# Softmax sums of an attention layer for two units at once, in four column strips

## The chip, the cores and the metric

The kernel runs on one core of a Trainium2 chip. The core has TensorE (matmuls, PE in the profile), VectorE (DVE), ScalarE (ACT), GpSimd (POOL) and SyncE (SP), which issues the DMAs. The metric is the device time of one execution in microseconds (us); lower is better. The kernel's time is a median over several runs. The profile is of one further execution.

## The reference

Eight images of 384 channels and 32 x 32 pixels pass four layers, each of the form x = x + layer(groupnorm(x)), in float32: a convolutional attention (layer 0), a mixture of four experts (layer 1), a quantised depthwise-separable convolution (layer 2) and a deformable attention (layer 3). The change is inside layer 3's attention. With 6 heads of 64 channels, 1024 queries (the pixels) and 256 keys (sampled positions), cut to what matters:

```python
    qh = q.reshape(B, NUM_HEAD, DIM_HEAD, H * W).transpose(0, 1, 3, 2)
    ...
    attn = jax.nn.softmax(jnp.einsum('bhqd,bhkd->bhqk', qh, k) * SCALE, axis=-1)
    out = jnp.einsum('bhqk,bhkd->bhqd', attn, v)
    out = out.transpose(0, 1, 3, 2).reshape(B, DIM, H, W)
    out = jnp.einsum('bchw,oc->bohw', out, proj_w) + proj_b[None, :, None, None]
```

So each query needs the sum of 256 exponentials, and the 64 outputs of its head are divided by that sum.

## The kernel before

The whole program is one launch. Layer 0 runs first, layer 1 of the images follows, and the last stage, in which the change lies, is a loop over the images b = 0 to 6: layers 2 and 3 of image b, written as a generator, are interleaved with layer 1 of image b + 1, which is cut into small units of TensorE work (groups of the ph matmuls, L1481, and of the y matmuls, L1502). Each `yield` of the generator adds its number to a budget, and for every 2.6 (`UNIT`) in it one unit of layer 1 is issued. The order in which instructions are issued is therefore the order on each engine. Image 6 runs beside image 7's layers 2 and 3, and image 7 (`last`) ends alone.

Layer 3's attention of an image is cut into six units: three head pairs `pr` times two halves `h` of 512 queries. One unit is made of these steps:

- `scores` (L1800): four matmuls, keys on the partitions and two heads side by side, into two large PSUM tiles.
- `exps` (L1817): two ScalarE exponentials of 128 x 1024, tiles p.
- p01 (L1862): GpSimd adds the two tiles, so that only 128 rows are left to be summed.
- `weigh` (L1826): four matmuls, p times v, into one PSUM bank pav; the two heads take 64 rows each. There is one such bank (`vbank`).
- tu (L1874): VectorE transposes pav in 32 x 32 blocks into an SBUF tile, which frees the bank.
- `sums` (L1839): two matmuls with a 128 x 64 block of ones, one for each head, write the sums into a bank pss (from `fbank`, three banks); each sum stands in 64 equal rows.
- `divide`: VectorE transposes pss (ts, L1847), takes the reciprocal of one column in each block (L1849, 128 x 16, kept in rec3), multiplies tu by it (L1850) and transposes the product into att (L1853).

The sums and the division of a unit are issued one unit late (`due3`): behind the next unit's weigh and, on VectorE, behind its tu. After the sixth unit come its own sums and division, and then the projection pf (L1929), x (L1937) and the output's DMA (L1944). Beside the tail VectorE starts the layer 1 of image b + 2: x<-o (L1427) with tiles o that a DMA loads (L1411) into buffers of the pool that also holds p and p01, and ScalarE makes h from x (L1430). Further VectorE work there is y's addition to x (L1508), its statistics (L106, L111) and x<-w0s (L1454).

rec3 keeps all reciprocals of all images; at the end of the program a check of their range reads it (outside the usual range a general version runs again).

Of the kernel before, what the change touches and what calls it, by code (L numbers as in the profile page):

```python
# [7 lines left out]
F32 = mybir.dt.float32  # L8
# [6 lines left out]
P = 128  # L15
KC = C // P
HALF = N // 2
# [38 lines left out]
def tile_kernel(ctx: ExitStack, tc: tile.TileContext, i: dict, out: bass.AP):  # L56
    nc = tc.nc
# [33 lines left out]
    ones = const.tile([P, P], F32, name="ones")  # L91
# [175 lines left out]
    with ExitStack() as pa:  # L267
# [7 lines left out]
        last = NK - 1  # L275
# [246 lines left out]
        for n, (u, kind, s) in enumerate(work):  # L522
            k, h = divmod(u, 2)
# [25 lines left out]
            else:  # L549
                two = [big(f"pk{n}_{r}") for r in range(2)]  # L550
                banks = [two[r // 2][:, r % 2 * HALF : (r % 2 + 1) * HALF] for r in range(4)]
                outs = [(t, 2 * r, 2) for r, t in enumerate(two)]
            if kind == "v":
                h, c = h + s, 0
# [5 lines left out]
            for p in passes:  # L560
                j, x = p
                c0, c1 = max(0, 1 - x), W - max(0, x - 1)
                for q in range(nq):
# [3 lines left out]
                    elif kind == "y":  # L567
                        g, j, w = s, q, slice(0, 64)
# [4 lines left out]
                    for r, rs in enumerate(quads):  # L573
                        nc.tensor.matmul(  # L574
                            banks[r][cols[q]].rearrange("p (h w) -> p h w", w=W)[:, :, c0:c1],
                            lhsT=cws[rs, c, 2 * h + g, x, w],
                            rhs=src[rs, :, c0 + x - 1 : c1 + x - 1],
                            start=(p == passes[0]), stop=(p == passes[-1]),
# [13 lines left out]
            for q in range(4):  # L592
                rows = quads[q]
                if kind == "y":
                    v, j = divmod(q, 2)
# [5 lines left out]
                else:  # L601
                    g, j = divmod(q, 2)
# [69 lines left out]
    with ExitStack() as pb:  # L672
# [192 lines left out]
        nxt = scores_of(*steps[0])  # L865
        todo.pop(0)()
        pav = None
        for n, (b, pr, h, kc) in enumerate(steps):
# [34 lines left out]
            if n + 1 < len(steps):  # L903
                nxt = scores_of(*steps[n + 1])
# [20 lines left out]
        for k in range(2):  # L925
            qs = slice(k * HALF // 2, (k + 1) * HALF // 2)
            for m in range(KC):
                for c in range(KC):
                    nc.tensor.matmul(
                        pos[m][:, qs], lhsT=wo0[:, c, m * P : (m + 1) * P],  # L930
                        rhs=atts[B - 1][:, c, HALF:][:, qs], start=(c == 0), stop=(c == KC - 1),
# [24 lines left out]
    _, sco, sho = sc_o  # L956
# [51 lines left out]
    with tc.If(redo > 0):  # L1008
        with ExitStack() as pb:
# [13 lines left out]
            with tc.For_i(0, B) as bi:  # L1023
# [11 lines left out]
                for t in range(NT8):  # L1035
                    pv = bank(f"pv_e{t}")
                    for c in range(KC):
                        nc.tensor.matmul(
                            pv[:, :C], lhsT=act[2][:, c, t * P : (t + 1) * P],
                            rhs=w_in[2][:, c, :], start=(c == 0), stop=(c == KC - 1),  # L1040
# [8 lines left out]
                for v in range(2):  # L1049
                    ts = qp.tile([P, NPAIR0, N], F32, tag=f"qk{v}", name=f"qk{v}_e")  # L1050
                    for pr in range(KC):
                        for h in range(2):
                            pq = bank(f"pq{v}_e{pr}_{h}")
                            for c in range(KC):
                                nc.tensor.matmul(
                                    pq, lhsT=w_in[v][:, c, pr * P : (pr + 1) * P],
                                    rhs=rows_of(act[v][:, c, :], h * H // 2, (h + 1) * H // 2) if v == 0
                                    else act[v][:, c, h * HALF : (h + 1) * HALF],
                                    start=(c == 0), stop=(c == KC - 1),
# [8 lines left out]
                for pr in range(NPAIR0):  # L1068
                    qt, kt = qks[0][:, pr, :], qks[1][:, pr, :]
                    for h in range(2):  # L1070
                        pav = bank(f"pav_e{pr}_{h}")
                        for j, r in enumerate(HR):
                            hd = 2 * pr + j
                            pt = qp.tile([P, NT8, HALF], F32, tag="pt", name=f"pt_e{pr}_{h}_{j}")
                            for qc in range(4):
# [3 lines left out]
                                for kh in range(2):  # L1079
# [3 lines left out]
                                        start=True, stop=True,  # L1083
# [3 lines left out]
                                p = pp.tile([P, N], F32, tag="p", name=f"p{nm}")  # L1087
# [14 lines left out]
                            for kc in range(NT8):  # L1102
# [5 lines left out]
                                    rhs=pt[:, kc, :],  # L1108
                                    start=(kc == 0),
                                    stop=(kc == NT8 - 1),  # L1110
# [49 lines left out]
    def fbank(name):  # L1160
        return ps_f.tile([P, HALF], F32, tag="f", name=name)
# [219 lines left out]
    om_dram = dram.tile([B, 3, NG * LS], F32, name="omd")  # L1381
    NU3 = 2 * NPAIR3
    rec3 = wd.tile([P, B * NU3, 16], F32, name="rec3")
    bad3 = wd.tile([P, 1], mybir.dt.int32, name="bad3")

    xs_img, started = {}, {}
# [209 lines left out]
    def layer3(pl, b, xt, put, general):  # L1596
# [196 lines left out]
        def scores(pr, h):  # L1793

            ss = []
            for kc in range(2):
                s = big(f"s3_{b}_{pr}_{h}_{kc}")
                for j in range(2):
                    r = slice(64 * j, 64 * j + 64)
                    nc.tensor.matmul(  # L1800
                        s[:, j * HALF : (j + 1) * HALF],
                        lhsT=kt[r, pr, kc * P : (kc + 1) * P],
                        rhs=q[r, pr, h * HALF : (h + 1) * HALF],
                        start=True, stop=True,
                    )
                ss.append(s)
            return ss

        def exps(u, ss):
            ps = []  # L1810
            for kc in range(2):
                nm = f"p3_{b}_{u}_{kc}"
                if last:
                    p = third(pl, 2 * (u % 2) + kc, nm).rearrange("p a n -> p (a n)")[:, :N]
                else:
                    p = pl.flat([P, N], nm)
                nc.scalar.activation(p, ss[kc], AF.Exp, scale=0.125)  # L1817
                ps.append(p)
            return ps
# [14 lines left out]
        if not general:  # L1834
            def sums(u, p01):

                pss = fbank(f"pss3_{b}_{u}")
                for j in range(2):
                    nc.tensor.matmul(  # L1839
                        pss[64 * j : 64 * j + 64, :], lhsT=ones[:, :64],  # L1840
                        rhs=p01[:, j * HALF : (j + 1) * HALF], start=True, stop=True,
                    )
                return pss

            def divide(pss, pr, h, u, tu):
                tss = pl.one([P, 16, 32], "ts", f"ts_{b}_{u}")
                nc.vector.transpose(tss.rearrange("p a b -> p (a b)"), pss)  # L1847
                rc = rec3[:, b * NU3 + u, :]
                nc.vector.reciprocal(rc, tss[:, :, 0])  # L1849
                nc.vector.tensor_tensor(  # L1850
                    tu, tu, rc.unsqueeze(2).to_broadcast([P, 16, 32]), ALU.mult
                )
                nc.vector.transpose(  # L1853
                    att[:, pr, h * HALF : (h + 1) * HALF], tu.rearrange("p a b -> p (a b)")
                )


            ps, due3 = exps(0, scores(*units[0])), None
            yield UNIT
            for u, (pr, h) in enumerate(units):  # L1860
                p01 = pl.flat([P, N], f"p01_{b}_{u}")
                nc.gpsimd.tensor_tensor(p01, ps[0], ps[1], ALU.add)  # L1862
                nxt = scores(*units[u + 1]) if u + 1 < NU3 else None
                if last and nxt:
                    nxt = exps(u + 1, nxt)
                pav = weigh(pr, h, ps)
                if due3:
                    pss = sums(due3[2], due3[4])
                if nxt:
                    ps = nxt if last else exps(u + 1, nxt)  # L1870

                tu = pl.one([P, NG * LS], f"om{u % 2}", f"tu_{b}_{u}")[:, :HALF]
                tu = tu.rearrange("p (a b) -> p a b", b=32)
                nc.vector.transpose(tu.rearrange("p a b -> p (a b)"), pav)  # L1874
                if due3:
                    divide(pss, *due3[:4])
                due3 = pr, h, u, tu, p01
                yield UNIT
                yield 0.0
            divide(sums(due3[2], due3[4]), *due3[:4])  # L1880
            yield 3.0
        else:
            for pr, h in units:
                pav = vbank(f"pav3_{b}_{pr}_{h}")
                for j in range(2):
                    r = slice(64 * j, 64 * j + 64)
                    nm = f"3_{b}_{pr}_{h}_{j}"
                    s = big(f"s{nm}").rearrange("p (a k) -> p a k", a=4)
                    for qc in range(4):
                        q0 = h * HALF + qc * P  # L1890
                        nc.tensor.matmul(
                            s[:, qc, :], lhsT=q[r, pr, q0 : q0 + P], rhs=kt[r, pr, :],
                            start=True, stop=True,
                        )
                    mx = small.tile([P, 4], F32, tag="mx4", name=f"mx{nm}")
                    nc.vector.reduce_max(mx, s, AX.X, negate=True)
                    nc.vector.tensor_scalar(mx, mx, 0.125, None, ALU.mult)
                    p = pl.flat([P, 4, LS], f"p{nm}")
                    rs = small.tile([P, 4], F32, tag="rs4", name=f"rs{nm}")
                    for qc in range(4):  # L1900
                        nc.scalar.activation(
                            p[:, qc, :], s[:, qc, :], AF.Exp, bias=mx[:, qc : qc + 1],
                            scale=0.125, accum_out=rs[:, qc : qc + 1],
                        )
                    nc.vector.reciprocal(rs, rs)
                    nc.vector.tensor_tensor(
                        p, p, rs.unsqueeze(2).to_broadcast([P, 4, LS]), ALU.mult
                    )
                    pt = pl.flat([P, 2, HALF], f"pt{nm}")
                    for kc in range(2):  # L1910
                        tp = fbank(f"tp{nm}_{kc}")
                        for qc in range(4):
                            nc.tensor.transpose(
                                tp[:, qc * P : (qc + 1) * P], p[:, qc, kc * P : (kc + 1) * P], ident
                            )
                        nc.vector.tensor_copy(pt[:, kc, :], tp)
                    hd = 2 * pr + j
                    for kc in range(2):
                        nc.tensor.matmul(
                            pav[r, :], lhsT=vt[:, kc, hd * 64 : (hd + 1) * 64], rhs=pt[:, kc, :],  # L1920
                            start=(kc == 0), stop=(kc == 1),
                        )
                nc.vector.tensor_copy(att[:, pr, h * HALF : (h + 1) * HALF], pav)
# [249 lines left out]
```

## Time and profile before

| quantity | value |
|---|---|
| median of 3 runs | 3491.53 us |
| lowest and highest run | 3490.93 and 3492.99 us |
| the profiled execution | 3494.72 us |
| its span | 3492.9 us |
| its mean granted TensorE clock | 0.987 |
| sums, L1839 | 192 records, median 592 ns |
| transpose of the sums, L1847 | 48, median 716 ns |
| reciprocal times tu, L1850 | 48, median 1300 ns, 672 to 1574 |
| addition of exponentials, L1862 | 48, mean 2355 ns |

A float32 matmul leaves two records, one for each pass; matmuls are pipelined, so that records overlap and the time of one is more than its share. In a line of the timeline the columns are the start in us from the span's start, the length of the group in us, engine, line of the kernel, operation, output and inputs, shapes, the number of records, and in brackets the idle time of the engine before it with what ended it. Times in the timeline are those of the profiled execution. A TensorE line with "128*64" has 128 rows of weights and 64 columns.

### The profile page before, as it was taken

The numbers are of one execution on the slowest core, as the hardware profiler recorded it, in microseconds if no ns is written. First come the engines' busy times: TensorE is split into PE (matmuls) and PEld (weight loads), VectorE is DVE, ScalarE is ACT, GpSimd is POOL, SyncE is SP. The second block draws the span as 40 slices with busy tenths as digits, with TensorE's granted clock in tenths as the row PEclk, the third lists the DMA queues.
The fourth block names the chain that finished last, engine by engine and source line by source line (L and its number), as shares of the span: only waits on it lengthen the run. The fifth ranks groups of instructions, "written<-read, shape, count | busy, mean of one in ns | idle before, by whom it ended". The sixth has DMA issues, their size and how long they took to land.

```text
span 3492.9 us, 44919 instructions
## 1 busy us (share of the span) xinstructions
PE 3384.1 (97%) x18599; PEld 1458.3 (42%) x18599; DVE 1696.7 (49%) x2881; ACT 1298.5 (37%) x1514; POOL 206.1 (6%) x231
## 2 busy tenths in 40 slices
PE   6999999999999999998999999999999999999888
PEld 2333434343434343443344445344453444534434
DVE  8942232323232323234366365663656637566573
ACT  5655544444444444433222323313233232232222
POOL 2100000000000000000000200102001020010112
PEclk9999999999999999999999999999999999999898
DMA  9972121212121212123500101101111011110000
GB/s 357 295 205 79 26 79 27 79 26 79 26 79 26 79 27 78 28 79 125 220 24 21 50 39 35 40 21 50 40 35 40 21 50 40 35 39 18 0 37 19
DMA packets 86259, 234.01 MB, mean 67 GB/s; under 512 B 21672, under 2 KB 21896, under 8 KB 79130
## 3 DMA queue, kind: packets, MB, share of 16 engines
q1 hardware_dynamic: 83882, 222.75, 19.9%
q10 hardware_dynamic: 1248, 4.72, 0.3%
q8 instruction: 150, 2.46, 0.3%
q0 software_dynamic: 912, 3.53, 0.3%
q14 instruction: 67, 0.55, 0.1%
HBM read 145.77 MB, written 75.59 MB: 63 GB/s over the span
## 4 chain that ended last, share of the span: by engine, by line
PE 41%; DVE 9%; DMA 1%; ACT 1%; POOL 0%; issue 0%; DVEq 0%; ACTq 0%; POOLq 0%; SPq 0%
PE y L1502 12%; PE ph L1481 10%; DVE y L1577 5%; PE pq L1622 4%; PE pw L1585 3%; PE pf L1929 3%; PE s L1800 2%; PE pav L1826 2%; DVE hd L1467 1%; DMA o<-o 1%; PE pk L1775 1%; PE pv L1784 1%; PE xsb L1761 1%; PE pss L1839 1%; PE plog L1231 1%; DVE off L1692 1%
## 5 line engine op out<-in xcount | busy, mean ns | idle before, releaser
L827 ACT ACTIVATE p<-s 128x1024 f32<-128x1024 f32 x512 | 496.3, 1021 | 365.7 <-PE s L820 365.5
L835 PE MATMUL pav<-p,vt 64*64 64x512 f32 x4096 | 494.7, 588 | 0.0
L1481 PE MATMUL ph<-h,w_sb 128*128 128x512 f32 x1104 | 486.8, 595 | 6.3 <-ACT h L1430 6.3
L1502 PE MATMUL y<-hd,w_sb 128*128 128x512 f32 x1080 | 488.7, 600 | 3.5 <-DVE hd L1467 3.5
L820 PE MATMUL s<-qk,qk 48*64 48x512 f32 x2944 | 355.1, 592 | 0.0
L1481 PEld LDWEIGHTS ph<-h,w_sb 128*128 128x128 f32 x1104 | 207.0, 190 | 267.5 <-issue 249.8
L1502 PEld LDWEIGHTS y<-hd,w_sb 128*128 128x128 f32 x1080 | 199.9, 191 | 248.2 <-issue 235.8
L835 PEld LDWEIGHTS pav<-p,vt 64*64 64x64 f32 x4096 | 168.2, 133 | 273.7 <-issue 273.4
L796 DVE COPY ta<-pav 128x512 f32<-128x512 f32 (+1 forms) x65 | 44.2, 682 | 475.5 <-PE pav L835 475.5
L1491 ACT ACTIVATE hd<-ph,b_sb 128x512 f32<-128x512 f32 x180 | 122.7, 682 | 312.7 <-PE ph L1481 312.7
L1577 DVE SCALAR_TENSOR_TENSOR y<-h,tap,y 128x961 f32<-128x961 f32 (+1 forms) x192 | 233.8, 1241 | 0.6
L574 PE MATMUL pk<-xs,cws_sb 32*32 32x496 f32 (+3 forms) x3840 | 179.4, 601 | 39.4 <-DMA xs<-in_xs_dram 24.8
L1692 DVE SCALAR_TENSOR_TENSOR off<-q,dw_sb,off 128x225 f32<-128x225 f32 (+3 forms) x432 | 211.9, 544 | 1.6
L820 PEld LDWEIGHTS s<-qk,qk 48*64 48x64 f32 x2944 | 109.1, 133 | 211.4 <-issue 190.5
L1817 ACT ACTIVATE p<-s 128x1024 f32<-128x1024 f32 x96 | 96.1, 1023 | 166.5 <-PE s L1800 141.7
L81 DVE COPY qk<-pq 128x512 f32<-128x512 f32 x46 | 31.8, 691 | 251.9 <-PE pq L258 251.9
L1467 DVE TENSOR_TENSOR hd<-hd,cb 128x512 f32<-128x512 f32 x180 | 122.3, 684 | 41.0 <-ACT hd L1491 40.8
L574 PEld LDWEIGHTS pk<-xs,cws_sb 32*32 32x32 f32 (+1 forms) x3840 | 77.7, 111 | 139.4 <-issue 54.0
L1585 PE MATMUL pw<-y,upw 128*128 128x512 f32 x288 | 129.0, 601 | 4.9 <-DVE y L1577 4.9
L1862 POOL TENSOR_TENSOR p<-p,p 128x1024 f32<-128x1024 f32 x48 | 113.0, 2355 | 349.3 <-ACT p L1817 349.3
L820 PE MATMUL s<-ql,ql 48*64 48x512 f32 x1024 | 128.3, 592 | 0.2 <-ACT p L827 0.2
L1929 PE MATMUL pf<-att,wp_sb 128*128 128x512 f32 x288 | 127.6, 598 | 0.5 <-DVE x L1937 0.5
(326 smaller groups left out, 3718.1 us busy)
## 6 DMA issues: line engine op xcount, KB each, us to landing
rqk<-y SPq DMA_DIRECT2D x96, 256.0 KB
g<-rqk SPq DMA_DIRECT2D x96, 256.0 KB
xs<-in_xs_dram SPq DMA_DIRECT2D x56, 384.0 KB
g<-rv SPq DMA_DIRECT2D x48, 256.0 KB
xh<-in_x_dram SPq DMA_DIRECT2D x48, 256.0 KB
f<-in_x_dram SPq DMA_DIRECT2D x24, 512.0 KB
f<-o SPq DMA_DIRECT2D x24, 512.0 KB
o<-ot SPq DMA_DIRECT2D x42, 256.0 KB
```

The costliest lines, as they stand in the source:

```text
L574: nc.tensor.matmul(banks[r][cols[q]].rearrange("p (h w) -> p h w", w=W)[:, :, c0:c1], lhsT=cws[rs, c, 2 * h + g, x, w], rhs=src[rs, :, c0 ...
L820: nc.tensor.matmul(s[64 * k : 64 * k + 64, j * HALF : (j + 1) * HALF], lhsT=kt[r, k0 : k0 + 64], rhs=qt[r, h * HALF : (h + 1) * HALF], sta ...
L827: nc.scalar.activation(p, s, AF.Exp, scale=scale)
L835: nc.tensor.matmul(pav[k][64 * j : 64 * j + 64, :], lhsT=vts[b % 2][r, kc, 2 * hd : 2 * hd + 2, :].rearrange("p a b -> p (a b)"), rhs=p[r, ...
L1467: nc.vector.tensor_tensor(hd, hd, state["cb"], ALU.mult)
L1481: nc.tensor.matmul(ph, lhsT=w1[:, e, c, dc * P : (dc + 1) * P], rhs=state["h1"][c], start=(c == 0), stop=(c == KC - 1),)
L1502: nc.tensor.matmul(y, lhsT=w2[:, e, dc, m * P : (m + 1) * P], rhs=state[h, k], start=(k == 0), stop=(k == NE * KC - 1),)
L1577: nc.vector.scalar_tensor_tensor(d, f, tap2[:, c, t : t + 1], d, ALU.mult, ALU.add)
L1585: nc.tensor.matmul(pw[h], lhsT=upw2[:, c, m * P : (m + 1) * P], rhs=y[c][:, hs], start=(c == 0), stop=(c == KC - 1),)
L1622: nc.tensor.matmul(pq[h], lhsT=wq3[:, c, m * P : (m + 1) * P], rhs=h3[h][:, c, :], start=(c == 0), stop=(c == KC - 1),)
L1692: nc.vector.scalar_tensor_tensor(d, f, dw3[:, t : t + 1], d, ALU.mult, ALU.add)
L1929: nc.tensor.matmul(pf[:, hs], lhsT=wp3[:, pr, m * P : (m + 1) * P], rhs=att[:, pr, hs], start=(pr == 0), stop=(pr == NPAIR3 - 1),)
```

## The change

For the images 0 to 6 the sums are made after every second unit, for two units at once. Four matmuls with a 128 x 32 block of ones write into four strips of 32 rows of one bank: two heads of two units. One transpose and one reciprocal serve both units; the reciprocal goes to a new 128 x 16 tile rc2, and eight copies of 32 x 16 bring its rows to where each unit's rows of tu need them: every strip is copied twice into rec3. Then follow multiply and transpose of each unit, as before (`turn`). The pair's sums and turns are issued after the second unit's `yield UNIT`, and so behind a unit of layer 1 if the budget holds one; the exponentials of the unit after a pair are issued behind them. Image 7 keeps the old order.

```diff
     rec3 = wd.tile([P, B * NU3, 16], F32, name="rec3")
+    rc2 = wd.tile([P, 16], F32, name="rc2")
...
+            def turn(rc, pr, h, tu):
+                nc.vector.tensor_tensor(
+                    tu, tu, rc.unsqueeze(2).to_broadcast([P, 16, 32]), ALU.mult
+                )
+                nc.vector.transpose(
+                    att[:, pr, h * HALF : (h + 1) * HALF], tu.rearrange("p a b -> p (a b)")
+                )
+
+            def divide_two(two):
+                pss = fbank(f"pss3_{b}_{two[0][2]}")
+                for k, (_, _, _, _, p01) in enumerate(two):
+                    for j in range(2):
+                        r = 64 * k + 32 * j
+                        nc.tensor.matmul(
+                            pss[r : r + 32, :], lhsT=ones[:, :32],
+                            rhs=p01[:, j * HALF : (j + 1) * HALF], start=True, stop=True,
+                        )
+                tss = pl.one([P, 16, 32], "ts", f"ts_{b}_{two[0][2]}")
+                nc.vector.transpose(tss.rearrange("p a b -> p (a b)"), pss)
+                nc.vector.reciprocal(rc2, tss[:, :, 0])
+                for k, (pr, h, u, tu, _) in enumerate(two):
+                    rc = rec3[:, b * NU3 + u, :]
+                    for j in range(2):
+                        for e in range(2):
+                            r = 64 * j + 32 * e
+                            nc.vector.tensor_copy(
+                                rc[r : r + 32], rc2[64 * k + 32 * j :][:32]
+                            )
+                    turn(rc, pr, h, tu)
+
             def divide(pss, pr, h, u, tu):
...
-                nc.vector.tensor_tensor(
-                    tu, tu, rc.unsqueeze(2).to_broadcast([P, 16, 32]), ALU.mult
-                )
-                nc.vector.transpose(
-                    att[:, pr, h * HALF : (h + 1) * HALF], tu.rearrange("p a b -> p (a b)")
-                )
-
-
-            ps, due3 = exps(0, scores(*units[0])), None
+                turn(rc, pr, h, tu)
+
+
+            ps, due3, two = exps(0, scores(*units[0])), None, []
...
-                if nxt:
+                if nxt and (last or u % 2 == 0):
                     ps = nxt if last else exps(u + 1, nxt)
...
-                due3 = pr, h, u, tu, p01
+                if last:
+                    due3 = pr, h, u, tu, p01
+                else:
+                    two.append((pr, h, u, tu, p01))
                 yield UNIT
+                if len(two) == 2:
+                    divide_two(two)
+                    two = []
+                    if nxt:
+                        ps = exps(u + 1, nxt)
                 yield 0.0
-            divide(sums(due3[2], due3[4]), *due3[:4])
+            if last:
+                divide(sums(due3[2], due3[4]), *due3[:4])
             yield 3.0
```

In the changed kernel the multiply stands in line 1847, the transpose into att in 1850, the pair's matmuls in 1859, its transpose, reciprocal and copies in 1864, 1865 and 1871, tu in 1900, and pf in 1964.

## The prediction

> **What bounds the kernel now.** I read the shares of the engines first, then the chain that ended last, then the timeline of TensorE in one attention stage, then VectorE's and GpSimd's beside it. From the page's first part and its chain:
>
> ```profile
> span 3492.9 us, 44919 instructions
> PE 3384.1 (97%) x18599; PEld 1458.3 (42%) x18599; DVE 1696.7 (49%) x2881; ACT 1298.5 (37%) x1514; POOL 206.1 (6%) x231
> PE 41%; DVE 9%; DMA 1%; ACT 1%; POOL 0%; issue 0%; DVEq 0%; ACTq 0%; POOLq 0%; SPq 0%
> ```
>
> TensorE is busy 97% of the span, so a matmul taken away shortens the run only if TensorE does not then wait. TensorE's timeline over the end of image 2's attention (start, length, engine, line, operation, count, idle before in brackets):
>
> ```profile
> 2428.12 2.84 PE L1502 MATMUL y<-hd,w_sb 128*128 128x512 f32 x6
> 2430.89 1.99 PE L1800 MATMUL s<-q,kt 64*128 64x512 f32 x8
> 2432.81 1.94 PE L1826 MATMUL pav<-p,vt 128*64 128x512 f32 x8
> 2434.57 1.03 PE L1839 MATMUL pss<-p,ones 128*64 128x512 f32 x4
> 2435.65 1.94 PE L1826 MATMUL pav<-p,vt 128*64 128x512 f32 x8
> 2437.39 1.92 PE L1839 MATMUL pss<-p,ones 128*64 128x512 f32 x8
> 2439.24 3.70 PE L1929 MATMUL pf<-att,wp_sb 128*128 128x512 f32 x8
> 2442.78 1.02 PE L1481 MATMUL ph<-h,w_sb 128*128 128x512 f32 x2
> 2444.92 1.13 PE L1481 MATMUL ph<-h,w_sb 128*128 128x512 f32 x2 [1.12 <-ACT h L1430]
> 2445.89 12.29 PE L1929 MATMUL pf<-att,wp_sb 128*128 128x512 f32 x28
> ```
>
> Groups follow without a gap except 1.12 us. One unit's sums (four records, two matmuls in two passes each) cost one slot: from one start to the next 2428.12 - 2427.16 = 0.96 us in the steady part, 1.92 for the two last units, of which 2 x 0.43 = 0.86 is streaming (592 ns of a record overlap its neighbour) and the rest is the change of shape. VectorE and GpSimd in a unit of image 1:
>
> ```profile
> 2200.84 2.35 POOL L1862 TENSOR_TENSOR p<-p,p 128x1024 f32<-128x1024 f32 x1 [5.06 <-ACT p L1817]
> ...
> 2200.54 0.72 DVE L1874 STREAM_TRANSPOSE tu<-pav 128x512 f32<-128x512 f32 x1 [3.47 <-PE pav L1826]
> 2201.40 0.72 DVE L1847 STREAM_TRANSPOSE ts<-pss 128x512 f32<-128x512 f32 x1
> 2202.15 0.25 DVE L1849 RECIPROCAL rec<-ts 128x16 f32<-128x16 f32 x1
> 2202.44 1.30 DVE L1850 TENSOR_TENSOR tu<-tu,rec 128x512 f32<-128x512 f32 x1
> 2203.77 0.71 DVE L1853 STREAM_TRANSPOSE att<-tu 128x512 f32<-128x512 f32 x1
> ```
>
> The multiply takes 1.30 us here and 0.68 after the last unit (2443.94). It ends 0.55 us after GpSimd's addition of the exponentials (2200.84 + 2.35 = 2203.19): while that addition runs, a VectorE operation with two inputs in SBUF stands still; transposes and reciprocals do not. And VectorE idles 3.47 us before a unit's turn, so in the steady part it has room.
>
> One more place shows what a long wait of TensorE costs, at the last image's attention:
>
> ```profile
> 3378.86 3.68 PE L1826 MATMUL pav<-p,vt 128*64 128x512 f32 x8 [4.23 <-DVE tu L1874]
> 3382.30 2.78 PE L1839 MATMUL pss<-p,ones 128*64 128x512 f32 x6
> ```
>
> After 4.23 us of waiting for VectorE the same eight records take 3.68 instead of 1.94 us.
>
> **What the Trainium skill says.** "TensorEngine Tiling (Array Packing)", Available Configurations and Key Properties: 128 rows by 32 columns makes four tiles that work independently, and a change of mode drains the array. The trace agrees: the gate logits (L1231), four 32-column strips, need 2.71 us for 24 records (1696.05 to the next group at 1698.76), which is 6 x 0.43 plus 0.13, and changes of shape cost 0.1 to 0.2. "VectorE: DVE Perf Modes", Two Vector instructions with no wait between them: an instruction whose input or output starts in another quadrant of 32 partitions than the last one's is held until all earlier ones have finished, and VectorE's second SBUF read interface is shared with GpSimd. The second half agrees with the multiplies above; shifted copies are not in this trace. "TensorE: Matmul & The Clock Gate", Part 1: an idle window of about 3.4 us halves the clock; the 4.23 us wait above agrees.
>
> **The change part by part**, for images 0 to 5 (one instruction order for all six), then image 6; image 7 keeps its code.
>
> 1. *Four strips.* Before, six slots per image. After: one slot for units 0 and 1, one for 2 and 3. In the third pair the first matmul of unit 4 is issued alone ahead of unit 5's pav, and the other three follow behind it: two slots again. So 6 become 4, not 3: 2 x 0.86 = 1.72 less, and all of it ahead of the point that matters (part 3). Two lone groups add a change of shape, so I take 1.6.
>
> 2. *VectorE's count.* Per pair one transpose (0.72) and one reciprocal (0.25) go; eight copies of 32 x 16 come. Nearest rows: L383's copy of 128x32, 160 ns; small steps of that kind are 0.09 to 0.10 us apart when independent and 0.19 when dependent. As all eight change quadrant, I take 0.17 each (0.10 to 0.25), 1.36 per pair against 0.97 saved: +0.4 per pair. In the steady part this lies in 3.47 us of idle time and costs nothing; without that cover it would cost its 0.4.
>
> 3. *The order on VectorE.* This decides. There is one vbank, so pav of a unit waits for the transpose tu (L1874) of the unit before. Before, tu of unit 4 followed directly on its pav. After, the whole turn of units 2 and 3 stands ahead of it: VectorE runs in order. Relative to the last y group (2428.12 in the view): y ends at 2.9 and the STT of L1508 takes to 3.6, transpose ts 4.35, with BATCH_NORM_AGGREGATE and the reciprocal 5.7, six copies 6.7, multiply of unit 2 7.4. GpSimd's addition for unit 5 starts about 7.2 (exponentials at about 5 and 6 behind s5) and ends about 9.7 (2.35, and some longer since unit 2's multiply already runs; one such addition took 2.52). If it stops what comes next, two copies, unit 2's transpose and unit 3's multiply are done at about 10.4, the transpose 11.1, tu of unit 4 11.85. TensorE, after y, the quad, s5, pav4 and one pss, is there at about 8.35 (before: 2435.65 - 2428.12 = 7.53). Stall about 3.5 us. Floor: copies at 0.10 and nothing stopped, 1.8. Ceiling: copies at 0.25, or copies and the first multiply stopped by GpSimd too, 4.8; from 3.4 the clock may halve as at 3378.86, where it took 3.68 - 1.94 = 1.7 for pav and about as much again behind it; at 3.5 I take it as not yet doing so.
>    Set against 1.6 saved ahead of it, pav5 starts (8.35 + 3.5) - 7.53 = 4.3 later counted from y, less the 1.6: +2.7 net (+1.0 to +4.0).
>
> 4. *The tail behind pav5.* Before, from pav5 to pf's end with the third ph is 2459.01 - 2435.65 = 23.4. After, pss is one slot shorter (-0.86), and the next image's x<-o load has its buffer early, since the stall gives the DMA its time: the 1.12 wait for h goes (-1.1). The turn of units 4 and 5 costs VectorE one transpose and reciprocal less, eight copies more, +0.4, behind which pf's second part waits, and I charge it with 0.2 (0 to 0.8), as ph groups fill most of it. Together -1.8 (-1.2 to -2.2).
>
>    The middle pair: pav3 waits for tu of unit 2, which VectorE has at about 11.5 against TensorE's 12.2 on the same kind of scale; no stall (0.9 if unit 0's multiply is stopped by GpSimd).
>
>    Sum per image: +2.7 - 1.8 = +0.9 (-1.0 to +2.8), times 6 = +5.4 (-6 to +17).
>
> 5. *Image 6.* It runs beside image 7's layer 2 and 3 with VectorE the limit in stretches (the chain shows DVE y L1577 at 5%). Three transposes and reciprocals go (-2.9), 24 copies come (+2.4 to +4), and the wait for pss moves off. Taken: -0.5 (-3.5 to +2), as most of it lies beside TensorE.
>
> 6. *The rest of the edits* (turn as a function, rc2, the exponentials emitted after the pair's turn, no divide after the loop) moves no DMA issue, and ScalarE's order stays; the exponentials wait for pav and the addition as before. GpSimd's queue has its additions in the old order, and SP's queue its DMAs; what moves there is only the time at which the x<-o load finds its buffer (part 4). Nothing, hidden by the same waits; if the exponentials did slip behind the pair's turn, the next pav would come later by up to the 1.0 us of one of them. rc2 has one buffer, but a pair's copies are long done when the next reciprocal comes.
>
> Sum: +5.4 - 0.5 = +5. The profiled execution took 3494.72 (span 3492.9 and 1.8 around it); the median shown is 3491.53, 3.2 below it; a difference carries over, so 3491.5 + 5 = 3496.5.
>
> **Rivals.**
> - *Clearly slower, by the clock.* The two copies and unit 2's multiply land behind GpSimd's addition, the stall reaches 4.5 and TensorE's clock halves for a window: per image +4.0 - 1.8 + 1.7 = +3.9, in half to all six images +12 to +23: about 3508. It decides from a stall of 3.4 us. It speaks for it that 7.4 against 7.2 is a near thing and that 3.5 is at the limit; against, that no window need fall on the wait whole, and that nothing like it shows at the waits of 1.1 us.
> - *Faster.* GpSimd comes too late to stop anything and the copies run at 0.10: stall 1.8, so per image +1.0 - 2.2 = -1.2, and image 6 gives -3: about -10, 3481. For it, the tail's wait for h; against, GpSimd's addition follows the exponentials, which the shorter sums bring earlier against VectorE's turn, not later. It decides from a stall below about 2 us.
> - *It doesn't do what it says.* The four strips do not run together with two different moving tiles: then a quad is two slots and nothing is saved, 6 x 1.7 more, 3507. The logits' 2.71 us speak against it.
>
> **How the numbers follow.** This kernel's measurement can tell about 0.2%, 7 us, from no change. Chances: the forecast (3487 to 3505) 0.55; clock 0.20; faster 0.17; not four at a time 0.08. Of the forecast's 0.55 about 0.19 lies above +7 and 0.02 below -7; of the faster case 0.03 lies inside. So slower 0.19 + 0.20 + 0.08 = 0.47, faster 0.14 + 0.02 = 0.16, same 0.37. The range 3482 to 3514 takes in the forecast's bounds, the faster case to its price and the clock case but for its upper end.
>
> **What would show it.** Per step: a pss group of eight records in about 0.96 us (1); copies L1871 of 0.1 to 0.25 (2); pav5 with a wait of about 3.5 for DVE tu in images 0 to 5, and multiplies longer than 1 us just ahead of it (3); no wait for h before the ph of the tail (4). Wrong if TensorE is stalled in the middle pair too, if the wait is under 2 us, or if its matmuls after the wait take twice as long.

## The result and the profile after

The changed kernel takes 3510.17 us (median of 6 runs, 3505.49 to 3511.07) against 3491.54 us before (6 runs, 3488.94 to 3492.99): the ratio is 1.0052, 95% interval 1.0042 to 1.0063. It is slower by 18.6 us, well outside what could be no change. The time lies in the predicted range, but not at the forecast of 3496.5: it came out near the rival in which TensorE's clock halves (3508).

TensorE in image 2 of the changed kernel, the same stretch as the timeline shown of before:

```profile
2430.53 2.84 PE L1503 MATMUL y<-hd,w_sb 128*128 128x512 f32 x6
2433.30 1.06 PE L1859 MATMUL pss<-p,ones 128*32 128x512 f32 x8
2434.30 1.99 PE L1801 MATMUL s<-q,kt 64*128 64x512 f32 x8
2436.22 1.94 PE L1827 MATMUL pav<-p,vt 128*64 128x512 f32 x8
2438.08 1.04 PE L1859 MATMUL pss<-p,ones 128*32 128x512 f32 x2
2442.90 3.63 PE L1827 MATMUL pav<-p,vt 128*64 128x512 f32 x8 [3.77 <-DVE tu L1900]
2446.47 1.06 PE L1859 MATMUL pss<-p,ones 128*32 128x512 f32 x6
...
2450.99 1.02 PE L1482 MATMUL ph<-h,w_sb 128*128 128x512 f32 x2
2451.85 0.28 PE L117 MATMUL gna_d<-mv_d,g_sb 128*128 128x2 f32 x2
2451.99 1.96 PE L1482 MATMUL ph<-h,w_sb 128*128 128x512 f32 x4
2453.79 12.18 PE L1964 MATMUL pf<-att,wp_sb 128*128 128x512 f32 x28
```

Eight records of sums now take one slot (2433.30 to 2434.30), so the four strips do run together. The third pair is split, two records ahead of unit 5's pav and six behind it. And pav of unit 5, which had started without a wait before, now waits 3.77 us for tu of unit 4, and then takes 3.63 us where the other pavs of the image take 1.94. The wait for h that stood in the tail before (1.12 us) is gone.

VectorE in the same stretch says where the wait is from:

```profile
2433.41 0.75 DVE L1509 SCALAR_TENSOR_TENSOR x<-y,yb,x 128x512 f32<-128x512 f32 x1 [2.05 <-PE y L1503]
2434.20 0.69 DVE L106 BATCH_NORM_STATS2 st_d<-x 128x6 f32<-128x512 f32 x1
2434.81 0.70 DVE L1864 STREAM_TRANSPOSE ts<-pss 128x512 f32<-128x512 f32 x1
2435.43 0.28 DVE L111 BATCH_NORM_AGGREGATE mv_d<-st_d 128x2 f32<-128x36 f32 x1
2435.63 0.19 DVE L1865 RECIPROCAL rc<-ts 128x16 f32<-128x16 f32 x1
2435.85 1.07 DVE L1871 COPY rec<-rc 32x16 f32<-32x16 f32 x6
2436.96 0.69 DVE L1847 TENSOR_TENSOR tu<-tu,rec 128x512 f32<-128x512 f32 x1
2437.68 2.42 DVE L1871 COPY rec<-rc 32x16 f32<-32x16 f32 x2
2440.13 0.71 DVE L1850 STREAM_TRANSPOSE att<-tu 128x512 f32<-128x512 f32 x1
2440.76 0.65 DVE L1847 TENSOR_TENSOR tu<-tu,rec 128x512 f32<-128x512 f32 x1
2441.45 0.71 DVE L1850 STREAM_TRANSPOSE att<-tu 128x512 f32<-128x512 f32 x1
2442.08 0.67 DVE L1900 STREAM_TRANSPOSE tu<-pav 128x512 f32<-128x512 f32 x1
```

Pav of unit 4 ends at about 2438.1, but its tu stands at the end of the turn of units 2 and 3 and comes at 2442.08. Six copies take 1.07 us; the two next ones take 2.42, of which the first has 2.23 (2437.68 to 2439.91). In that time GpSimd does unit 5's addition, which ends at 2439.88:

```profile
2437.54 2.34 POOL L1888 TENSOR_TENSOR p<-p,p 128x1024 f32<-128x1024 f32 x1 [4.25 <-ACT p L1818]
```

The last view shows the clock. The records of the changed kernel have five stretches of half clock in images 0 to 5, each 3.41 us long, beginning at 2221.11, 2442.98, 2664.84, 2886.71 and 3108.58 us: one within half a microsecond of the start of unit 5's pav in each of the images 1 to 5. They are 221.87 us apart, which is 65 times 3.413. The view is of windows of that length, around the wait in image 0 and in image 1 (the columns are the window, its length, busy us and instructions of TensorE, weight loads, VectorE, ScalarE and GpSimd, then the granted TensorE clock, the DMA share and GB/s). The windows of image 0 lie 65 lengths before those of image 1:

```profile
1995.84:1999.25 3.41, 1.56 (x6) 0.14 (x2) 3.33 (x5) 0.00 (x0) 2.31 (x1) 1.00 0.49 150
1999.25:2002.66 3.41, 1.48 (x8) 0.57 (x8) 1.74 (x3) 0.00 (x0) 0.00 (x0) 1.00 0.01 4
2217.70:2221.11 3.41, 0.08 (x1) 0.00 (x0) 3.33 (x6) 0.00 (x0) 0.85 (x1) 1.00 0.49 154
2221.11:2224.52 3.41, 2.95 (x8) 0.85 (x8) 0.32 (x1) 0.00 (x0) 0.00 (x0) 0.50 0.00 0
```

The wait is the same in both (3.78 and 3.79 us). In image 0 it is spread over two windows, in each of which TensorE is still busy for about 1.5 us, and the clock stays at 1.00; in image 1 it fills one window but for 0.08 us, and the next runs at 0.50. Half of 3.41 us, at most 1.7 us, is lost in each of the images 1 to 5.

From the starts of TensorE's records the time can be laid out by stage (us; mean of images 0 to 5, s0 being the first scores matmul of an image):

| stage | before | after |
|---|---|---|
| s0 to pav of unit 5 | 38.26 | 41.52 |
| pav of unit 5 to the end of pf | 22.46 | 21.37 in image 0, 22.99 in images 1 to 5 |
| end of pf to the next s0 (images 0, 2, 4) | 159.02 | 157.49 |
| image 6, s0 to image 7's s0 | 126.02 | 126.84 |
| s0 of image 0, from the span's start | 1957.73 | 1959.65 |

The second and third row are to be read together: in the changed kernel the stretch up to the end of pf holds one ph group and a gna more than before, about 1 us, and the stage behind it so much less. Images 0 to 5 are longer by 12.0 us together, image 6 by 0.8 and image 7 by 0.3. The 1.9 us ahead of image 0 are in code that is the same in both; in the profiles of the experiments image 0 starts anywhere between 1955.7 and 1960.5 us. The spans differ by 15.1 us and the medians by 18.6, since the profiled execution of before was 3.2 us above its median and that of the changed kernel 0.4 below its own; in later comparisons single runs of the kernel before lay between 3486.8 and 3497.2.

### The profile page after: what moved, and what is told of

It is laid out like the page before. It is cut to its first block, busy times and chain, and to the rows that moved or that the text cites. A ratio compares the mean times of both kernels' runs of the same rounds, so it can differ in the third digit from the quotient of the medians.

```text
span 3508.0 us, 45034 instructions
## 1 busy us (share of the span) xinstructions
PE 3379.0 (96%) x18599; PEld 1452.3 (41%) x18599; DVE 1708.7 (49%) x3007; ACT 1296.5 (37%) x1514; POOL 205.8 (6%) x231
## 4 chain that ended last, share of the span: by engine, by line
PE 48%; DVE 4%; issue 0%; ACT 0%; DMA 0%; DVEq 0%; POOL 0%; POOLq 0%; ACTq 0%
PE ph L1482 14%; PE y L1503 14%; PE pq L1623 4%; PE pf L1964 3%; PE pw L1586 3%; PE pav L1827 2%; PE s L1801 2%; PE pk L1776 1%; PE pv L1785 1%; PE xsb L1762 1%; DVE rec L1871 1%; PE plog L1231 1%; DVE y L1578 1%; DVE off L1693 1%; PE xs L1762 0%; PE px L1646 0%
```

## The experiments

Each was timed against the kernel before, which had medians of 3492.16 us (no_add5, no_copies, fill_wait, pairs_01_45), 3492.66 (pair_23_only, pair_01_only, four_copies, four_copies_01_45) and 3490.65 (eight_together). Unless said otherwise an edit is made to the changed kernel.

**no_add5.** Is it GpSimd's addition that stops the copies?

```diff
...
-                nc.gpsimd.tensor_tensor(p01, ps[0], ps[1], ALU.add)
...
+                if u == 5 and not last:
+                    p01 = ps[0]
+                else:
+                    nc.gpsimd.tensor_tensor(p01, ps[0], ps[1], ALU.add)
```

> The changed kernel, but GpSimd's addition for unit 5 is left out in images 0 to 6, so that the sums of unit 5 cover only the first 128 of 256 keys. Theory A (the pair's turn ahead of unit 4's tu makes the stall, and GpSimd's addition lengthens it by stopping two copies for 2.42 us): the two copies take about 0.35 us, TensorE's wait before pav of unit 5 falls from 3.77 to about 1.7 us, the clock no longer halves behind it, and the time falls by (2.07 + 1.4) x 6, about 21, to about 3489 us. Rival B (the eight copies' own time makes the stall, GpSimd does not matter): the wait stays above 3.3 us and the time within 4 us of 3510.

Measured: 3488.56 us, ratio to before 0.9989 (0.9983 to 0.9996). The source line of the copies (durations in ns: least, median, greatest), first in the changed kernel, then in this one, and this one's wait:

```profile
L1871 DVE COPY rec<-rc x168: 118/166/2357, 1979.6 to 3402.0; 32x16 f32<-32x16 f32 x168
```

```profile
L1871 DVE COPY rec<-rc x168: 120/166/173, 1978.0 to 3379.8; 32x16 f32<-32x16 f32 x168
```

```profile
2435.16 1.94 PE L1827 MATMUL pav<-p,vt 128*64 128x512 f32 x8 [1.71 <-DVE tu L1903]
```

With the addition gone no copy takes more than 173 ns, the wait falls from 3.77 to 1.71 us, by 2.06 as expected, and pav is back at 1.94 us. Rival B falls. What is left, 1.7 us, is the joined turn itself, its order and its copies; the next run parts these two.

**no_copies.** The copies' own time, and what it pushes behind the addition.

```diff
-                nc.vector.reciprocal(rc2, tss[:, :, 0])
                 for k, (pr, h, u, tu, _) in enumerate(two):
                     rc = rec3[:, b * NU3 + u, :]
-                    for j in range(2):
-                        for e in range(2):
...
+                    nc.vector.reciprocal(rc, tss[:, :, 0])
                     turn(rc, pr, h, tu)
```

> The changed kernel without the eight copies of a pair: the reciprocal is written straight into rec3 once for each of the two units, so that most rows of tu are multiplied with the sum of another head or unit. Theory A: both multiplies of units 2 and 3 now start before GpSimd's addition for unit 5 does and are not stopped; the wait before pav of unit 5 falls by the copies' 1.4 and the 2.07 of the stop, less 0.2 to 0.7 for the second reciprocal and the order, to about 0.5 to 1.0 us; the clock does not halve; about 3485 us. Rival B (only the copies' own time): the wait falls by 1.4 - 0.25 to about 2.6 us, and the time to about 3500.

Measured: 3469.34 us, ratio 0.9933 (0.9919 to 0.9947). The wait is not 0.5 to 1.0 us but nil, and the time is 16 us under the expectation. In image 2 both multiplies are over at 2424.42, before GpSimd's addition starts at 2424.82, and tu of unit 4 is done at 2426.24, just before pav of unit 5 starts at 2426.38. So the order alone does not stall TensorE here; the copies' own 1.4 us, and the stop into which they bring the turn, do.

From one image's s0 to the next, image 0 takes 216.59 us, against 220.39 in image 0 of the changed kernel, where the clock was full too. The 3.80 us between them lie ahead of pav of unit 5 (37.72 us behind s0, against 41.52). What stands behind it takes as long in both, 178.87 us: the stretch to the end of pf is 0.86 us shorter and the next stage 0.86 longer, since one ph group has moved. In this tail the copies cost nothing. The rest of the difference from the changed kernel is the clock (8.1 us in five images), image 6 (120.71 us, 6.1 less) and 3.7 us ahead of image 0, in code that is the same; the expectation had neither of the last two. Image 6 is not the copies' price alone: it is 4.0 us shorter in no_add5 as well, which has all of them. What shortens it was not followed up.

**fill_wait.** What the clock costs.

```diff
+                if u == 5 and not last:
+                    fill = fbank(f"fill3_{b}")
+                    for i in range(4):
+                        nc.tensor.matmul(
+                            fill, lhsT=ident, rhs=q[:, 0, :HALF], start=True, stop=True
+                        )
                 pav = weigh(pr, h, ps)
```

> The changed kernel with four more matmuls of 128x128 by 128x512 ahead of pav of unit 5 in images 0 to 6, into a bank that nothing reads: they keep TensorE at work for 3.4 us of its wait. Theory A (the wait lets the clock halve, 1.7 us in five of six images of the profile): pav of unit 5 starts when it did and takes 1.94 us in all images, the granted clock stays at 1.00 in the 10 us behind it, and the time falls by 5 to 6 times 1.5, to about 3501 us. Rival C (the clock is lower there for another reason, as a load of TensorE over a longer stretch): pav of unit 5 still takes 3.4 us or more and the time stays at 3510 or rises by the matmuls that do not fit.

Measured: 3505.6 us, ratio 1.0036 (1.0022 to 1.0049). TensorE's timeline of image 2:

```profile
2437.89 3.70 PE L1895 MATMUL fill<-q,ident_sb 128*128 128x512 f32 x8
2442.72 1.94 PE L1827 MATMUL pav<-p,vt 128*64 128x512 f32 x8 [1.12 <-DVE tu L1906]
2444.58 1.06 PE L1859 MATMUL pss<-p,ones 128*32 128x512 f32 x8
2445.58 3.70 PE L1970 MATMUL pf<-att,wp_sb 128*128 128x512 f32 x8
```

Pav of unit 5 starts where it did (41.52 us behind s0) and takes 1.94 us in images 0 to 5, so the longer pav is due to TensorE's idleness and not to its load over a longer stretch: Rival C falls. The gain is 4.6 us and not the 9 expected. The fill also changed the order: the third pair's sums stay whole behind pav, VectorE's turn of units 4 and 5 comes after other work, and TensorE waits 0.69 us for att in the tail of each of the images 0 to 5, where the changed kernel has no such wait. In the profile, what stands behind the start of pav takes 179.83 us in image 2, against 180.57 in the changed kernel at the lowered clock and 178.87 in its image 0, so about 1 us of the 1.7 goes to the new order. The clock's own price is therefore read from the lengths of pav (3.38 to 3.63 us for 1.94) and the windows, 1.4 to 1.7 us per image, and not from this time.

**pairs_01_45.** Only the middle pair taken back: units 2 and 3 go through sums and divide, a unit late.

```diff
+            pairs = () if last else (0, 1, 4, 5)
...
-                if nxt and (last or u % 2 == 0):
+                if nxt and (u not in pairs or u % 2 == 0):
...
-                if last:
+                due3 = None
+                if u not in pairs:
                     due3 = pr, h, u, tu, p01
                 else:
                     two.append((pr, h, u, tu, p01))
...
-            if last:
+            if due3:
                 divide(sums(due3[2], due3[4]), *due3[:4])
```

> Pairs only for units 0 and 1 and for 4 and 5; units 2 and 3 get their sums and turns singly, a unit late, as in the kernel before. Theory A: tu of unit 4 stands ahead of unit 3's turn again, so pav of unit 5 does not wait; two slots of sums less per image (2 x 0.9) and the tail shorter by 1 to 1.5 us (no wait for h); six images by about 3 us less than before, 3474 us (3468 to 3484). Rival D (what the change loses lies in the tail with its copies or in image 6, not in the middle pair): about as slow as the changed kernel, at least 3495.

Measured: 3486.94 us, ratio 0.9979 (0.9969 to 0.9989): 23 us less than the change, 5 less than before, and 13 more than expected. The wait before pav of unit 5 is gone and s0 to pav is 37.54 us, 0.72 less than before. The stage behind pf is 1.5 us shorter, as in the changed kernel. But from pav to the end of pf it took 23.2 us (before 22.5), and VectorE shows why:

```profile
2435.28 0.25 DVE L1865 RECIPROCAL rc<-ts 128x16 f32<-128x16 f32 x1
2436.86 1.28 DVE L1428 SCALAR_TENSOR_TENSOR x<-o,bnsc_out,x 128x1024 f32<-128x1024 f32 x1 [1.34 <-DMA o<-o]
2438.06 1.06 DVE L1871 COPY rec<-rc 32x16 f32<-32x16 f32 x6
2439.16 0.69 DVE L1847 TENSOR_TENSOR tu<-tu,rec 128x512 f32<-128x512 f32 x1
2439.88 0.35 DVE L1871 COPY rec<-rc 32x16 f32<-32x16 f32 x2
2440.26 0.71 DVE L1850 STREAM_TRANSPOSE att<-tu 128x512 f32<-128x512 f32 x1
```

The wait for the load of o, 1.34 us, is here as it was before. The load is issued as pav of unit 5 starts, here (2429.71 and 2429.69) as before (2435.68 and 2435.65); in the changed kernel it is issued 4.7 us ahead of it (2438.23 and 2442.90), during TensorE's stall. The stall thus helped the tail of the changed kernel, but a short tail does not need it: no_copies, with no stall, has no wait for h and takes the same 178.87 us from there on as image 0 of the changed kernel. Behind the wait for o, in this run, the copies stand on the path to att of unit 4, which comes 10.6 us after pav of unit 5 starts (9.5 before), and TensorE waits 0.86 us for it. (This stretch also holds one ph group and a gna more than before, about 1 us, which is most of what the stage behind pf is shorter by.)

**pair_23_only and pair_01_only.** The same edit with other pairs in the list.

```diff
-            pairs = () if last else (0, 1, 4, 5)
+            pairs = () if last else (2, 3)
```

> Only units 2 and 3 as a pair; units 0, 1, 4 and 5 singly, as in the kernel before. Theory A: the wait before pav of unit 5 and the lower clock behind it are there as in the changed kernel (about 3.8 us and 1.4 us for each of six images), while the two slots of sums ahead of it are not saved and only the wait for h in the tail goes: per image about 3.8 + 0.4 + 1.4 - 1.5 = +4, so about 3515 us, slower than the change with all three pairs. Rival D (the loss is in the other pairs or in image 6): between 3490 and 3500 us.

> Only units 0 and 1 as a pair, the others singly. Theory A: one slot of sums less per image ahead of pav of unit 5 (0.72 us by the stage times of the kernel with pairs 01 and 45), nothing late on VectorE since a y group stands between, no change in the tail: about -5 us, 3486.5 us. Rival D (the copies of any pair cost time on the path): no gain or a loss, 3491 to 3496 us.

Measured: with units 2 and 3 alone 3522.47 us, ratio 1.0085 (1.0071 to 1.0099), with units 0 and 1 alone 3487.71 us, 0.9990 (0.9981 to 0.9998). The waits of TensorE for tu in the first of them (us in total, times, longest):

```profile
PE pav L1827 <- DVE tu L1901: 27.6, 7, 4.2
```

The middle pair alone costs 30 us, 7 more than expected and more than the whole change, since all six images have the wait and its pav takes 2.64 to 3.68 us in each, and nothing is saved ahead of it. The first pair alone has no new wait and gives about 5 us: 0.72 us for each of six images by the stage times, 4.3, and something in image 6. So the loss sits in the middle pair. Rival D falls.

**four_copies.** The strips in another order, r = 64j + 32k, so that each unit's sums already stand in two of its four row groups.

```diff
-                        r = 64 * k + 32 * j
+                        r = 64 * j + 32 * k
...
-                nc.vector.reciprocal(rc2, tss[:, :, 0])
+                rcs = [rec3[:, b * NU3 + t[2], :] for t in two]
+                for rc in rcs:
+                    nc.vector.reciprocal(rc, tss[:, :, 0])
+                for k, rc in enumerate(rcs):
+                    for j in range(2):
+                        to, fr = 64 * j + 32 * (1 - k), 64 * j + 32 * k
+                        nc.vector.tensor_copy(rc[to : to + 32], rc[fr : fr + 32])
...
```

Then both multiplies, then both transposes.

> All three pairs, but the strips are ordered so that each unit's reciprocal already stands in two of its four row groups: one reciprocal for each unit straight into rec3 and four copies for a pair instead of one reciprocal and eight copies; both multiplies ahead of both transposes. Theory A: VectorE's chain for units 2 and 3 is shorter by 0.6 us and both multiplies start before GpSimd's addition for unit 5: the wait before pav of unit 5 is about 1.0 to 1.3 us, no lower clock, the tail shorter by about 1 us than in the changed kernel: about 3479 us (3474 to 3486), less than before. Rival E (four copies still bring the second multiply behind GpSimd's addition): wait 2.7 to 3.3 us, about 3492.

Measured: 3480.74 us, ratio 0.9970 (0.9958 to 0.9981). VectorE in image 2, then GpSimd and TensorE:

```profile
2425.18 0.30 DVE L1867 RECIPROCAL rec<-ts 128x16 f32<-128x16 f32 x2
2425.52 0.72 DVE L1871 COPY rec<-rec 32x16 f32<-32x16 f32 x4
2426.27 1.29 DVE L1873 TENSOR_TENSOR tu<-tu,rec 128x512 f32<-128x512 f32 x2
2427.49 1.30 DVE L1877 STREAM_TRANSPOSE att<-tu 128x512 f32<-128x512 f32 x2
2428.71 0.67 DVE L1905 STREAM_TRANSPOSE tu<-pav 128x512 f32<-128x512 f32 x1
```

```profile
2427.10 2.68 POOL L1893 TENSOR_TENSOR p<-p,p 128x1024 f32<-128x1024 f32 x1 [4.25 <-ACT p L1818]
```

```profile
2429.53 1.94 PE L1827 MATMUL pav<-p,vt 128*64 128x512 f32 x8 [0.84 <-DVE tu L1905]
```

Both multiplies (1.29 us for two) have begun when the addition starts at 2427.10, and it is now the addition that is held up, 2.68 us instead of 2.34. The wait is 0.84 us. All three pairs, with half the copies and in this order, are faster than the kernel before. Rival E falls.

**four_copies_01_45.** The same copies and the list of pairs_01_45.

> The same four copies, pairs only for units 0 and 1 and for 4 and 5. Theory A: no wait before pav of unit 5, and VectorE's turn of units 4 and 5, which the projection waits for, is shorter by 0.6 us or more: about 5 us less than with eight copies, 3482 us (3476 to 3486). Against four_copies it saves the wait of about 1.1 us per image and gives one slot of 0.9 us back and the early load of the next image: within 5 us of it.

Measured: 3477.03 us, ratio 0.9959 (0.9945 to 0.9972): the fastest version found that computes everything, 33 us under the changed kernel and 16 under the one before, and within its band. s0 to pav of unit 5 is 37.54 us and the tail 20.98 to 21.62.

**eight_together.** The eight copies of the changed kernel, all ahead of the multiplies, which stand together as in four_copies. It parts the order from the number of copies.

```diff
-                for k, (pr, h, u, tu, _) in enumerate(two):
-                    rc = rec3[:, b * NU3 + u, :]
+                rcs = [rec3[:, b * NU3 + t[2], :] for t in two]
+                for k, rc in enumerate(rcs):
...
-                    turn(rc, pr, h, tu)
+                for rc, (pr, h, u, tu, _) in zip(rcs, two):
+                    nc.vector.tensor_tensor(
+                        tu, tu, rc.unsqueeze(2).to_broadcast([P, 16, 32]), ALU.mult
+                    )
+                for pr, h, u, tu, _ in two:
+                    nc.vector.transpose(
...
```

> The changed kernel with its eight copies, but all eight ahead of both multiplies, and both multiplies ahead of both transposes. Theory A (what counts is whether VectorE's chain is done with its SBUF-to-SBUF work when GpSimd's addition for unit 5 starts): the eighth copy ends about 0.3 us before the addition starts, the first multiply slips in and the second is stopped until the addition ends; the wait before pav of unit 5 stays at 3.4 to 3.9 us and the time is 3502 to 3511 us. Rival F (the order alone, both multiplies back to back, is what freed four_copies): the second multiply is not stopped, the wait is about 1.5 us and the time about 3487 us.

Measured: 3512.54 us, ratio 1.0062 (1.0048 to 1.0076), one or two us above the band. VectorE, then GpSimd:

```profile
2437.72 1.44 DVE L1871 COPY rec<-rc 32x16 f32<-32x16 f32 x8
2439.18 3.44 DVE L1875 TENSOR_TENSOR tu<-tu,rec 128x512 f32<-128x512 f32 x2
```

```profile
2439.41 2.67 POOL L1895 TENSOR_TENSOR p<-p,p 128x1024 f32<-128x1024 f32 x1 [4.25 <-ACT p L1818]
```

The first multiply begins 0.23 us ahead of the addition, the second is stopped, and the two take 3.44 us instead of 1.29; the wait before pav is 3.59 us. Rival F falls: four copies less, about 0.7 us, decide over 2.1 us of standing still and over the clock, which here falls in all six images.

## Why the prediction was right and where it was off

*Part 1, the strips:* right. A quad is one slot and the third pair is split. The size was a little off: one slot saved brings 0.72 us (pair_01_only, pairs_01_45), not 0.86. Most of the difference is a change of shape: pav had been followed by sums of its own shape (1.76 us from start to start before) and is now followed by another shape (1.87).

*Part 2, the copies:* 0.17 us each was forecast, 166 ns is the median, and six take 1.07 us. In the forecast's working unit 3's multiply waits for GpSimd (10.4 is the addition's end at 9.7 and one multiply), and a stopped copy was left for the upper bound. What was stopped is a copy, and no_add5 shows it. "The Trainium skill", VectorE: DVE Perf Modes, Two Vector instructions with no wait between them, names VectorE's second SBUF read interface as shared with GpSimd, for operations with two SBUF inputs and for those that run in a 2-port mode; the copies' 2357 ns against 166 would fit the second case, but no trace here shows in which mode a copy runs.

*Part 3, the order:* right, and in its size helped by chance: the stopped copy made VectorE's turn longer than reckoned, but the addition ended earlier, 9.35 us after the start of y (2439.88 - 2430.53) where 9.7 was reckoned. The wait was forecast at 3.5 us and is 3.77; pav of unit 5 against s0 was forecast at +2.7 and is +3.26, of which 0.27 is the wait and 0.27 the smaller slots.

*The step that failed* is in the same part: "at 3.5 I take it as not yet doing so", of the clock that halves. It did so in five of six images of the profile. From the tails, 22.99 - 21.37 = 1.62 us each, 8.1 together: more than the forecast had for the whole change. One of the prediction's own signs of being wrong came true with it: pav after the wait takes nearly twice as long. The mechanism stood there as a rival with a price of 1.7 us per image, in half to all images, and a point of decision at 3.4 us. Against it stood that no window need fall on the wait whole. Image 0 shows just that, but the next five images met the windows in the same place, and so the clock fell in each; over the three kernels with such a stall (3.77 us here, 3.90 in pair_23_only, 3.59 in eight_together) it fell in 17 of 18 images. The chance of 0.20 was too low for a forecast that itself lay beyond the point of decision.

*Part 4, the tail:* at full clock it is -1.09 and -1.53, -2.6 us, against -1.8 forecast. The wait for h went as forecast, and the load was early, as forecast. But it takes no such stall for the wait to go: four_copies, with a stall of 0.84 us, and no_copies, with none, have no wait for h either. The copies on the path to att, charged with 0.2 us, cost nothing in the changed kernel (no_copies takes as long there) and 0.86 us in pairs_01_45. The 0.8 us by which the tail beats the forecast are not assigned.

*Part 5, image 6:* forecast -0.5, measured +0.8.

The sum by these measures: six images of 3.26 - 1.09 - 1.53 = +0.64, that is 3.8 where 5.4 was forecast, and 8.1 for the clock, together the 12.0 of the profile; image 6 adds 0.8. The remaining 5.8 us to the medians' 18.6 are the 1.9 us ahead of image 0, the 0.3 in image 7, and the 3.2 and 0.4 by which the profiled executions lay off their medians; no experiment was aimed at them. Without the clock the images add 3.8 + 0.8 = 4.6 us, near the forecast's 5 and no better than the kernel before; that this fits so well is in part chance, since the wait and the tail were off by like amounts in opposite directions. So is the nearness to the rival's 3508: it was priced at 3.9 us per image, the images took 2.0, and the 5.8 us made up for it.

## What to carry to other kernels

Work that is batched on one engine is late work: before joining the turns of two units, look which small operation stands behind the joined turn on the same engine, and which single buffer it frees; here one transpose of 0.7 us, queued behind a joined turn, held TensorE for 3.8 us. Look also what another engine does in the time into which the longer chain reaches: four copies more, about 0.7 us, made the wait 3.59 us instead of 0.84 (eight_together against four_copies), because they brought a multiply into GpSimd's 2.4 us. And when a stall comes out longer than one stretch of the lowered clock, here 3.41 us, price the drop as the likely case: it came behind 17 of 18 such waits.

## What the runs showed of the hardware beyond that

- A copy with a single SBUF input, 32 x 16, was stopped by a GpSimd addition until that ended: up to 2357 ns for 166. The other way round, an addition that starts while VectorE multiplies takes 2.67 to 2.68 us for 2.34.
- The same wait of TensorE does not always lower the clock, and its length alone does not tell. In each of the eleven profiles all stretches of lowered clock begin a whole number of 3.413 us apart, to within 0.01 us. Cut into windows on that grid, images 0 to 5 of all profiles have 17 windows at full clock in which TensorE was busy for 38% or less, and the clock was halved behind every one of them; behind the other full-clock windows, with 43% or more, it never was. Beside image 6 the border is less sharp: there a window with 54% was followed by the lower clock in three profiles, the changed kernel's among them.
